# Two layers of attention on one core: both layers divide by the softmax sum by way of DMA, with the product of the second layer on VectorE

## The chip, the core and the metric

The kernel runs on one core of a Trainium2 chip, in one launch. The metric is the time of an execution on the device in microseconds (us). An execution that is profiled has a time of its own, and the span of its records, from the first instruction to the last, is a little shorter. The engines are named as in the profile: PE is TensorE (matmuls and transposes), PEld its loads of weights, DVE is VectorE, ACT is ScalarE, POOL is GpSimd, SP is SyncE, which here only issues DMAs. PE works at full or at reduced clock; the profile gives the clock that was granted as a share of the full one.

## The reference

The input x has B = 2 sequences of T = 2048 tokens with D = 256 features, in fp32. Two layers follow one another, each of the same shape:

```python
for layer in (0, 1):
    xn = layernorm(x)
    s  = attention(xn)          # 16 heads of 16 features, then W_o and b_o (layer 0: + xn)
    g  = silu(ffn(xn))
    x  = x + s * g
```

The attention of layer 0 is full: every query sees all 2048 keys, with scale 1/16. The attention of layer 1 is local: query i sees key j where |i - j| <= 64, with scale 1/4. In both, softmax(q k^T) v is computed per head, the heads are put side by side and multiplied with W_o. The ffn of layer 0 is a mixture of eight products of projections with a running sum over the tokens; that of layer 1 is one linear map plus eight gated low-rank ones. The change leaves the ffn parts alone.

## The kernel before

All activations are held with features on the 128 partitions and tokens along the free axis. The 256 features are two chunks (NC = 2), the tokens of one sequence are four blocks of TB = 512 (NB = 4). The kernel has four stages: preparation, layernorm and ffn of layer 0 (0 to 475 us), attention of layer 0 (to 2141), layernorm and ffn of layer 1 (to 2246), attention of layer 1 (to the end).

**Attention (L402, called once for each layer).** The 16 heads are four groups (g) of NG = 4. A group of four heads stands in one tile: each head has 32 partitions (HP), of which 16 (HD) hold its features. In the tiles of q and k the row after these features is used too: in k it holds ones, in q minus the largest score of that query, so that the score matmul (32 rows deep) already yields the score less its maximum. In v a column of ones is added, so that the weighted sum also yields, in row 16 of each head's 32, the softmax sum by which the result has to be divided.

The work is cut into 32 items (b, g, n): one sequence, one group of heads, one block of 512 queries. An item has U steps: 16 in layer 0 (one per 128 keys), 2 in layer 1 (one per 256 queries with their neighbouring keys). For an item the maxima come first: PE computes scores into `sq` (L599), DVE reduces them (L611 in layer 0; in layer 1 L606, which adds a mask and takes the maximum in one pass). `place_max` (L630) turns the maxima with a PE transpose (`pmx`, L636), negates them on DVE (`row`, L638), and four DMAs put them into the q tile (L640). LEAD = 3 steps later the scores are computed again, `sk` (also L599), ACT takes the exponential (L615), in layer 1 POOL masks four tiles a step (affine select, L620), and DEL steps later (1 in layer 0, 2 in layer 1) `weigh` (L648) multiplies with v: 16 or 24 small matmuls into `acc` (L662), which ACT copies and, in layer 0, POOL adds up into `av` (L673).

**The order of the work** is written out by hand. The main loop (L824) goes through the steps; in each it issues the scores of the second pass of step s and of the first pass of step s + U + LEAD, the weighted sum of step s - DEL, and then what a table holds for step s. The table is filled by `at(step, function, item)` (L778). Instructions wait for each other only where they use the same tile. Before step 0 the loop has U + LEAD steps with first-pass scores alone; in these the query, key and value jobs of the second sequence (`pp`, L446 and L459) are spread, after an eighth of them has been issued ahead of the loop. Some instructions are pinned with `keep_in_program_order`: a scheduler orders the others of an engine.

**q and k** are computed for all heads of a sequence (`keys_queries`, L442), written to DRAM (`qd`, L451) and fetched by group (`fetch`, L509): for q and k each four DMAs of 16 rows (L519), and one more that sets row 16 of each head in q to zero (L521, from `zd`). POOL memsets have given the tiles their ones and zeros beforehand (L427 on).

**The division in layer 0** (L716 to L753): at hops of 0, 2, 4, 5, 7 and 11 steps after an item, `compact` stores the four rows of softmax sums in DRAM (`rd`) and moves the 4 x 16 rows of values into `xn`, where the features of two groups fill 128 partitions; `invert` loads the sums as 128x16 (`dn`) and takes the reciprocal on DVE (L733); `spread` writes it back to DRAM and loads it as 64x512, each row 16 times (`recb`, L744); `divide` multiplies on POOL (L753). For the last group of a block `project` (L756) follows at hop 13: 4 matmuls with W_o in two halves (`pr`, L761), product with the gate on DVE (`upd`, L766), sum into x on POOL (L767).

**The division in layer 1** (L681 to L706): `normalize` transposes av on PE in four pieces (`tr`, L687), so that tokens stand on partitions and a softmax sum is one column per head; DVE takes the reciprocal (L689) and multiplies (L690) into a tile with tokens on partitions. For the last group of a block `features` transposes two chunks back with four PE transposes each (`of`, L703), ACT copies them to SBUF (L705), and `project` follows.

Of the kernel before, what the change touches and what calls it, by code (L numbers as in the profile page):

```python
# [13 lines left out]
ALU = mybir.AluOpType  # L14
# [23 lines left out]
def two_layers(ctx: ExitStack, tc: tile.TileContext, a, out):  # L38
# [114 lines left out]

    with tc.tile_pool(name="fw", bufs=1) as fw:
# [90 lines left out]
        nc.vector.memset(ones, 1.0)  # L245

# [155 lines left out]
    def attention(A, scale, local, final):  # L402
# [14 lines left out]
        with ExitStack() as st:  # L417
            pool = lambda name, bufs, **kw: st.enter_context(tc.tile_pool(name=name, bufs=bufs, **kw))
            kq, vp, dr = pool("kq", 1), pool("vp", 1), pool("dr", 1, space=bass.MemoryType.DRAM)
            qd = dr.tile([2, B, D, T], F32, name="qd")  # L420
# [3 lines left out]
            zd = dr.tile([NG, T], F32, name="zd")  # L424

            rd = [[dr.tile([NG, TB], F32, name=f"rd{i}{k}", tag=f"rd{i}{k}") for k in range(2)] for i in range(2)]
            for t in qs:  # L427
                nc.gpsimd.memset(t, 0.0)
            for t in vs + ks:
                nc.gpsimd.memset(t, 1.0)  # L430
            nc.sync.dma_start(out=zd, in_=qs[0][:NG, :])
# [10 lines left out]
            def keys_queries(b, n, i, hf, bank, place):  # L442
                w, bias = ((A["k"], A["bk"]), (A["q"], A["bq"]))[i]
                ps = bank()
                for c in range(NC):
                    nc.tensor.matmul(  # L446
                        ps, w[:, c, bass.ts(hf, P)], xn[b][:, c, bass.ts(n, TB)], start=(c == 0), stop=(c == NC - 1)
                    )
                sb = place()
                nc.scalar.activation(sb, ps, AF.Identity, bias=bias[:, hf : hf + 1])  # L450
                nc.sync.dma_start(out=qd[i, b, bass.ts(hf, P), bass.ts(n, TB)], in_=sb)  # L451
# [57 lines left out]
            def fetch(bg, lo=0, hi=T):  # L509

                if bg >= B * NG:
                    return
                b, g = divmod(bg, NG)
                k0, k1 = max(lo - PAD, 0), (T if hi == T else hi - PAD)
                for i, t in ((1, qs[bg % 2]), (0, ks[bg % 2])):
                    to, s = (slice(lo, hi), slice(lo, hi)) if i else (slice(PAD + k0, PAD + k1), slice(k0, k1))
                    for j in range(NG):
                        h = g * NG + j
                        nc.sync.dma_start(out=t[j * HP : j * HP + HD, to], in_=qd[i, b, h * HD : (h + 1) * HD, s])  # L519

                nc.sync.dma_start(out=qs[bg % 2][HD:P:HP, lo:hi], in_=zd[:, lo:hi])  # L521
# [108 lines left out]
            def place_max(i):  # L630

                b, g, n = items[i]
                q = tiles(i)[0]
                mx, _ = part.pop(i)
                ps = pm.tile([NG * TT, P], F32, name="pmx", tag="m")
                nc.tensor.transpose(ps, mx.rearrange("p j t -> p (j t)"), ident)  # L636
                row = mp.tile([NG * TT, P], F32, name="row", tag="row")
                nc.vector.tensor_scalar(row, ps, -1.0, None, ALU.mult)  # L638
                for j in range(NG):
                    nc.sync.dma_start(  # L640
                        out=q[j * HP + HD : j * HP + HD + 1, bass.ts(n, TB)].rearrange("o (t c) -> o t c", c=P),
                        in_=row[j * TT : (j + 1) * TT, :],
                    )
# [4 lines left out]
            def weigh(i, u, es):  # L648

                b, g, n = items[i]  # L650
                if u == 0:
                    avs[i] = op.tile([P, TB], F32, name="av", tag="av", bufs=2)
# [22 lines left out]
            def heads(b, n):  # L675

                return xn[0 if local else b].rearrange("p c t -> p (c t)")[:, bass.ts(n, TT * D)].rearrange(
                    "p (t h w) -> p t h w", h=H, w=HD
                )

            def normalize(i):  # L681

                b, g, n = items[i]
                av = avs.pop(i)
                ps = pm.tile([P, TT, NG, HP], F32, name="tr", tag="m")
                for t in range(TT):
                    nc.tensor.transpose(ps[:, t].rearrange("p j w -> p (j w)"), av[:, bass.ts(t, P)], ident)  # L687
                rec = op.tile([P, TT, NG], F32, name="rec", tag="rec", bufs=2)
                nc.vector.reciprocal(rec, ps[:, :, :, HD])  # L689
                nc.vector.tensor_tensor(  # L690
                    heads(b, n)[:, :, g * NG : (g + 1) * NG, :], ps[:, :, :, :HD],
                    rec[:, :, :, None].to_broadcast([P, TT, NG, HD]), ALU.mult,
                )

            feats = {}

            def features(i, c):

                b, g, n = items[i]
                ot = heads(b, n).rearrange("p t h w -> p t (h w)")  # L700
                ps = pm.tile([P, TB], F32, name="of", tag="m")
                for t in range(TT):
                    nc.tensor.transpose(ps[:, bass.ts(t, P)], ot[:, t, bass.ts(c, P)], ident)  # L703
                f = op.tile([P, TB], F32, name="f", tag=f"f{c}", bufs=2 if local else 1)
                nc.scalar.copy(f, ps)  # L705
                feats[b, n, c] = f  # L706

            def together(b, g, n):


                lo = g % 2 * NG * HD
                return xn[b][lo : lo + NG * HD, g // 2, bass.ts(n, TB)]

            divs = {}

            def compact(i):  # L716

                b, g, n = items[i]
                av = avs.pop(i)
                nc.sync.dma_start(out=rd[i % 2][0], in_=av[HD:P:HP, :])  # L720
                for j in range(NG):
                    nc.sync.dma_start(out=together(b, g, n)[j * HD : (j + 1) * HD, :], in_=av[j * HP : j * HP + HD, :])

            def flat(d):
                return d.rearrange("j (r e) -> (j r) e", r=P // NG)

            def invert(i, step):

                if step == 0:
                    divs[i] = op.tile([P, NG * TB // P], F32, name="dn", tag="dn", bufs=2)  # L730
                    tc.keep_in_program_order(nc.sync.dma_start(out=divs[i], in_=flat(rd[i % 2][0])))
                else:
                    tc.keep_in_program_order(nc.vector.reciprocal(divs[i], divs[i]))  # L733

            def spread(i, step):

                b, g, n = items[i]
                if step == 0:
                    tc.keep_in_program_order(nc.sync.dma_start(out=flat(rd[i % 2][1]), in_=divs[i]))
                    return  # L740
                recb = op.tile([P, TB], F32, name="recb", tag="recb", bufs=2)
                lo = g % 2 * NG * HD
                for j in range(NG):
                    tc.keep_in_program_order(nc.sync.dma_start(  # L744
                        out=recb[lo + j * HD : lo + (j + 1) * HD, :], in_=rd[i % 2][1][j, :].partition_broadcast(HD)
                    ))
                divs[i] = recb[lo : lo + NG * HD, :]

            def divide(i):

                b, g, n = items[i]
                tc.keep_in_program_order(
                    nc.gpsimd.tensor_tensor(together(b, g, n), together(b, g, n), divs.pop(i), ALU.mult)  # L753
                )

            def project(i, oc):  # L756
# [3 lines left out]
                for c in range(NC):  # L760
                    nc.tensor.matmul(  # L761
                        pr, A["o"][:, c, bass.ts(oc, P)], feats[b, n, c] if local else xn[b][:, c, cols],
                        start=(c == 0), stop=(c == NC - 1),
                    )
# [13 lines left out]
            def at(s, f, *args):  # L778
                after.setdefault(s, []).append((f, args))

            for i, (b, g, n) in enumerate(items):
                at(i * U - LEAD, place_max, i)
                end = (i + 1) * U
                if local:
                    at(end + DEL, normalize, i)
                    if g == NG - 1:
                        for c in range(NC):
                            at(end + DEL + 1 + c, features, i, c)
                        for oc in range(NC):
                            at(end + DEL + 3 + oc, project, i, oc)  # L790
                else:

                    for r, (f, *step) in enumerate(
                        ((compact,), (invert, 0), (invert, 1), (spread, 0), (spread, 1), (divide,))
                    ):
                        at(end + DEL + (0, 2, 4, 5, 7, 11)[r], f, i, *step)
                    if g == NG - 1:
                        for oc in range(NC):
                            at(end + DEL + 13 + oc, project, i, oc)
# [152 lines left out]
def _attn_arrays(l, wq, wk, wv, bq, bk, bv, wo_t, bo):  # L952

    cols = lambda v: np.asarray(v).reshape(NC, P).T
# [4 lines left out]
        f"wo{l}": np.asarray(wo_t).T,  # L959
        f"bq{l}": cols(bq),  # L960
        f"bk{l}": cols(bk),
        f"bv{l}": cols(bv),
# [56 lines left out]
```

## Time and profile before

| | us |
|---|---|
| median of 3 runs | 2621.34 (2620.46 to 2621.35) |
| the profiled execution | 2619.84 |
| span of its records | 2618.1 |
| PE busy | 2570.3 (98%) |
| DVE busy | 1671.5 (64%) |
| ACT busy | 1641.1 (63%) |
| POOL busy | 894.9 (34%) |
| mean granted clock of PE | 0.991 of full |

The times of an engine are those in which it was busy with an instruction other than waiting or issuing. A line of a group reads: line, engine, operation, result and operands with their shapes, count, then busy time and the mean of one in ns, then the idle time of the engine just before them and who ended it. A line of the chain reads: start in us, duration in us, engine, result and line, count; the chain is the work that ended last, followed back from the end, so each piece is what the next one waited for.

### The profile page before, as it was taken

To read this page: it belongs to the slowest core of one execution; us is meant where nothing else is said; L and a number is where in the kernel's file an instruction comes from. 1 tells how busy PE (TensorE), PEld (TensorE's weight loads), DVE (VectorE), ACT (ScalarE), POOL (GpSimd) and SP (SyncE) were. 2 spreads that over 40 slices of the span, in tenths; PEclk is the share of its full clock that TensorE was granted. 3 is DMA by queue.
4 is the path that set the end of the run, shared out by engine and by line. 5 is a ranking of instruction groups with operands and counts; after the bars stand their busy time and mean duration, and the time that the engine had idled before them with its cause. 6 is when DMAs were issued, how large, how long until landed. Compare 5 with 4: busy or idle time off the path is not lost.

```text
span 2618.1 us, 49275 instructions
## 1 busy us (share of the span) xinstructions
PE 2570.3 (98%) x19060; PEld 1099.6 (42%) x19060; DVE 1671.5 (64%) x2753; ACT 1641.1 (63%) x3200; POOL 894.9 (34%) x845
## 2 busy tenths in 40 slices
PE   8999999999999999999999999999999978999999
PEld 5444444543333333333333333333333324558776
DVE  4133332167888888888777888888888523228884
ACT  5300000228888888888778888888888854236655
POOL 0000000203444444444444444444444430206666
PEclk9999999999999999999999999999999989989999
DMA  4031110410001010010010010010000012411120
GB/s 150 3 88 45 53 45 32 99 64 4 8 12 19 8 24 9 6 25 8 6 25 8 6 25 8 6 27 6 8 8 6 10 30 35 96 67 39 46 58 35
DMA packets 58857, 82.08 MB, mean 31 GB/s; under 512 B 24160, under 2 KB 29152, under 8 KB 57040
## 3 DMA queue, kind: packets, MB, share of 16 engines
q1 hardware_dynamic: 56576, 77.36, 12.3%
q8 instruction: 150, 2.46, 0.4%
q10 hardware_dynamic: 2048, 1.58, 0.2%
q14 instruction: 83, 0.68, 0.1%
HBM read 52.22 MB, written 21.95 MB: 28 GB/s over the span
## 4 chain that ended last, share of the span: by engine, by line
PE 97%; DVE 1%; ACT 1%; DMA 0%; issue 0%; POOL 0%; SPq 0%; POOLq 0%; ACTq 0%; DVEq 0%
PE sk L599 25%; PE acc L662 22%; PE sq L599 19%; PE pp L446 4%; PE py L377 4%; PE po L357 4%; PE px L373 4%; PE ph L263 2%; PE pr L761 2%; PE pp L459 2%; PE psf L199 1%; PE po L909 1%; PE tr L687 1%; PE xb L127 1%; PE po L389 1%; PE xt L104 1%
## 5 line engine op out<-in xcount | busy, mean ns | idle before, releaser
L611 DVE TENSOR_REDUCE part<-sq 128x2 f32<-128x1024 f32 x1024 | 1206.7, 1220 | 304.2 <-PE sq L599 303.7
L615 ACT ACTIVATE e<-sk 128x512 f32<-128x512 f32 x2048 | 1062.7, 615 | 214.9 <-PE sq L599 192.2
L599 PE MATMUL sk<-q,k 32*128 32x512 f32 (+2 forms) x5632 | 1149.7, 533 | 0.6 <-ACT e L615 0.4
L599 PE MATMUL sq<-k,q 32*128 32x512 f32 (+2 forms) x5120 | 1140.8, 572 | 3.2 <-DVE part L611 1.7
L673 POOL TENSOR_TENSOR av<-av,more 128x512 f32<-128x512 f32 x480 | 607.7, 1266 | 961.2 <-ACT more L672 961.1
L599 PEld LDWEIGHTS sk<-q,k 32*128 32x128 f32 x5632 | 532.3, 184 | 581.1 <-ACT e L615 490.9
L662 PE MATMUL acc<-e,v 128*32 128x512 f32 x4096 | 550.6, 605 | 0.0
L599 PEld LDWEIGHTS sq<-k,q 32*128 32x128 f32 x5120 | 412.5, 184 | 28.0 <-DVE part L611 14.0
L672 ACT COPY more<-acc 128x512 f32<-128x512 f32 x480 | 287.8, 600 | 3.8 <-PE acc L662 1.7
L662 PEld LDWEIGHTS acc<-e,v 128*32 128x32 f32 x4096 | 82.4, 108 | 391.5 <-ACT e L615 387.0
L393 ACT ACTIVATE gt<-po 128x512 f32<-128x512 f32 x16 | 9.5, 596 | 324.6 <-PE po L389 324.6
L606 DVE CUSTOM_DVE_ANT_0 seen<-sq,mask 128x256 f32<-128x256 f32 (+1 forms) x512 | 177.4, 411 | 41.5 <-PE sq L599 32.8
L399 POOL TENSOR_TENSOR x<-x,up 128x512 f32<-128x512 f32 x16 | 20.2, 1264 | 416.4 <-DVE up L396 416.4
L620 POOL TENSOR_SCALAR_AFFINE_SELECT xn<-xn 128x512 f32<-128x512 f32 x172 | 103.1, 635 | 119.3 <-ACT xn L615 117.4
L381 DVE TENSOR_TENSOR xs<-we,px 128x512 f32<-128x512 f32 x64 | 43.8, 685 | 135.4 <-PE px L373 135.4
L373 PE MATMUL px<-xn,FV 128*128 128x512 f32 x256 | 121.2, 595 | 0.0
L377 PE MATMUL py<-cum,FW 128*128 128x512 f32 x256 | 120.5, 593 | 0.6 <-DVE cum L346 0.6
L615 ACT ACTIVATE xn<-sk 128x512 f32<-128x512 f32 x172 | 90.1, 601 | 48.2 <-PE sk L599 12.9
L357 PE MATMUL po<-pr,UO 128*128 128x512 f32 x256 | 119.0, 592 | 0.0
L383 DVE TENSOR_TENSOR pr<-xs,py 128x512 f32<-128x512 f32 x64 | 44.0, 687 | 62.4 <-PE py L377 62.2
L766 DVE TENSOR_TENSOR upd<-gt,pr 128x512 f32<-128x512 f32 x32 | 22.0, 687 | 86.0 <-PE pr L761 79.5
L357 PEld LDWEIGHTS po<-pr,UO 128*128 128x128 f32 x256 | 48.6, 190 | 61.2 <-issue 60.7
(169 smaller groups left out, 1683.2 us busy)
## 6 DMA issues: line engine op xcount, KB each, us to landing
we<-wd SPq DMA_DIRECT2D x128, 128.0 KB
qd<-sb SPq DMA_DIRECT2D x48, 256.0 KB
k<-qd SPq DMA_DIRECT2D x40, 128.0 KB
q<-qd SPq DMA_DIRECT2D x40, 128.0 KB
x<-in_x SPq DMA_DIRECT2D x8, 512.0 KB
q<-row SPq DMA_DIRECT2D x256, 2.0 KB
xn<-av SPq DMA_DIRECT2D x128, 32.0 KB
recb<-rd SPq DMA_DIRECT2D x128, 32.0 KB
```

What stands on the lines that cost most here:

```text
L357: nc.tensor.matmul(po[oc], UO[:, ch, bass.ts(oc, P)], pr, start=(ch == 0), stop=False)
L373: nc.tensor.matmul(px, FV[:, c, bass.ts(ch, P)], xn[b][:, c, cols], start=(c == 0), stop=(c == NC - 1))
L377: nc.tensor.matmul(py, FW[:, c, bass.ts(ch, P)], cum[:, c, :], start=(c == 0), stop=(c == NC - 1))
L446: nc.tensor.matmul(ps, w[:, c, bass.ts(hf, P)], xn[b][:, c, bass.ts(n, TB)], start=(c == 0), stop=(c == NC - 1))
L599: nc.tensor.matmul(o, lhs, rhs, start=True, stop=True)
L606: nc.vector.tensor_tensor_reduce(seen[:, lo:hi], sq[:, d, t * 2 * P + lo : t * 2 * P + hi], mask[:, lo:hi], 1.0, LOWEST, ALU.add, ALU.max, ...
L611: nc.vector.tensor_reduce(pt[:, pair[0] : pair[1] + 1, t, kb], sq, AX.X, ALU.max)
L615: nc.scalar.activation(e, t, AF.Exp, scale=scale)
L620: nc.gpsimd.affine_select(out=e[:, :, c, :], in_=e[:, :, c, :], compare_op=ALU.is_ge, fill=0.0, base=0, pattern=[[0, 4], [sign, P]], chann ...
L662: nc.tensor.matmul(acc[hp[j], o : o + hi - lo], vs[b][:, kt, vcols(g, j)], es[j][:, lo:hi], start=(r == 0), stop=(r == len(parts) - 1), sk ...
L672: nc.scalar.copy(more, acc)
L673: nc.gpsimd.tensor_tensor(avs[i], avs[i], more, ALU.add)
```

## The change

Layer 1 now divides as layer 0 does, by DMA, and layer 0's DMAs are put together into fewer ones:

- `away` stores the whole tile av (four heads of 32 rows) in DRAM; `compact` loads the softmax sums from there as 128x16 and the 64 rows of values into `xn`, with one DMA each; `invert` takes the reciprocal, `write` stores it, `spread` loads it 16 times over with one DMA, `divide` multiplies. That one DMA can place the four heads, the rows are taken value by value (first value of the four heads, second value of the four heads, and so on): the rows of W_o and the value bias are put in this order on the host (`apart`).
- The hops are 0, 1, 3, 4, 5, 7 with the projection at 8 in layer 1, and 0, 2, 4, 5, 7, 11 with the projection at 13 in layer 0.
- The product stands on DVE in layer 1 and on POOL in layer 0.
- The last item of layer 0 and the last three of layer 1 are divided on PE: `last_there` is the former transposition with reciprocal and product, `last_back` turns the result back with four matmuls against the identity, and ACT copies 64 rows into `xn`. The projection follows at hop 2.
- `qd` is made once, for both layers, with 32 rows per head; eight DMAs of 1 MB in the preparation fill the rows beside the features with ones (k) and zeros (q). `fetch` takes q and k of a group with one DMA each, of 128 rows. The memsets of the q and k tiles on POOL, and `zd`, go.
- `place_max` stores the maxima with one DMA in place of four. `av` has three buffers in layer 1.

```diff
@@ preparation
+            for i, t in ((0, ones), (1, zeros)):
+                for half in range(NC):
+                    nc.sync.dma_start(
+                        out=qd[i, b, bass.ts(half, H // NC), HD:, :], in_=t[:, None, :].to_broadcast([P, NB, TB])
+                    )
...
@@ fetch
-                    for j in range(NG):
-                        h = g * NG + j
-                        nc.sync.dma_start(out=t[j * HP : j * HP + HD, to], in_=qd[i, b, h * HD : (h + 1) * HD, s])
-
-                nc.sync.dma_start(out=qs[bg % 2][HD:P:HP, lo:hi], in_=zd[:, lo:hi])
+                    nc.sync.dma_start(out=t[:, to], in_=qd[i, b, bass.ts(g, NG), :, s].rearrange("h w t -> (h w) t"))
...
@@ place_max
-                for j in range(NG):
-                    nc.sync.dma_start(
-                        out=q[j * HP + HD : j * HP + HD + 1, bass.ts(n, TB)].rearrange("o (t c) -> o t c", c=P),
-                        in_=row[j * TT : (j + 1) * TT, :],
-                    )
+                nc.sync.dma_start(out=q[HD:P:HP, bass.ts(n, TB)].rearrange("j (t c) -> j t c", c=P), in_=row)
...
@@ division
+            def away(i):
+                pin(nc.sync.dma_start(out=ad[i % 3].rearrange("j w f -> (j w) f"), in_=avs.pop(i)))
...
+            def compact(i):
+                divs[i] = op.tile([P, NG * TB // P], F32, name="dn", tag="dn", bufs=3)
+                pin(nc.sync.dma_start(out=divs[i], in_=flat(ad[i % 3][:, HD, :])))
+                pin(nc.sync.dma_start(out=together(*items[i]), in_=ad[i % 3][:, :HD, :].rearrange("j d f -> d j f")))
+            def invert(i):
+                pin(nc.vector.reciprocal(divs[i], divs[i]))
+            def write(i):
+                pin(nc.sync.dma_start(out=flat(rd[i % 3]), in_=divs[i]))
+            def spread(i):
+                lo = items[i][1] % 2 * NG * HD
+                recb = op.tile([P, TB], F32, name="recb", tag="recb", bufs=2)
+                divs[i] = recb[lo : lo + NG * HD, :]
+                pin(nc.sync.dma_start(out=divs[i], in_=rd[i % 3][None, :, :].to_broadcast([HD, NG, TB])))
+            def divide(i):
+                b, g, n = items[i]
+                pin(
+                    (nc.vector if local else nc.gpsimd).tensor_tensor(together(b, g, n), together(b, g, n), divs.pop(i), ALU.mult)
+                )
...
+            def last_back(i):
+                b, g, n = items[i]
+                lo = g % 2 * NG * HD
+                o = divs.pop(i).rearrange("p t d j -> p t (d j)")
+                ps = pm.tile([P, TB], F32, name="of", tag="m")[lo : lo + NG * HD, :]
                 for t in range(TT):
+                    nc.tensor.matmul(ps[:, bass.ts(t, P)], o[:, t], ident, start=True, stop=True)
+                nc.scalar.copy(together(b, g, n), ps)
...
@@ table
+                hops = (0, 1, 3, 4, 5, 7, 8) if local else (0, 2, 4, 5, 7, 11, 13)
+                steps = (away, compact, invert, write, spread, divide)
+                if i >= len(items) - (3 if local else 1):
+                    hops, steps = (0, 1, 2), (last_there, last_back)
+                for hop, f in zip(hops, steps):
+                    at(end + DEL + hop, f, i)
+                if g == NG - 1:
+                    for oc in range(NC):
+                        at(end + DEL + hops[-1] + oc, project, i, oc)
```

## The prediction

> **What bounds the kernel now.** I read the busy shares and the chain that ended last first, to see which engine has to get shorter.
>
> ```profile
> PE 2570.3 (98%) x19060; PEld 1099.6 (42%) x19060; DVE 1671.5 (64%) x2753; ACT 1641.1 (63%) x3200; POOL 894.9 (34%) x845
> PE 97%; DVE 1%; ACT 1%; DMA 0%; issue 0%; POOL 0%; SPq 0%; POOLq 0%; ACTq 0%; DVEq 0%
> ```
>
> The end is set by PE (TensorE) nearly everywhere, so the change pays where it takes instructions from PE, closes a gap in PE's work or ends a stretch at half clock. The division of layer 0 (475 to 2141 us) already runs on DMA and POOL beside PE; only its last item shows. So I looked at layer 1 and at the last item of layer 0, each by its own stretch of the chain.
>
> Layer 1, a steady stretch of the chain:
>
> ```profile
> 2379.75 1.07 PE acc L662 x24
> 2380.83 0.59 PE tr L687 x4
> ...
> 2386.90 1.08 PE acc L662 x24
> 2387.98 0.59 PE tr L687 x4
> ```
>
> The four transposes of an item stand on the chain, at 0.59 us. From one to the next is 7.15 us; over eleven items, from the second copy into av at 2370.28 to the one at 2449.16, it is 7.17. But VectorE is close behind. Groups of 2340 to 2450:
>
> ```profile
> L606 DVE CUSTOM_DVE_ANT_0 seen<-sq,mask 128x256 f32<-128x256 f32 (+1 forms) x232 | 80.1, 410 | 11.0 <-PE sq L599 7.7 <-PE sk L599 3.1 <-issue 0.2
> L690 DVE TENSOR_TENSOR xn<-tr,rec 128x256 f32<-128x256 f32 x12 | 5.1, 424 | 0.4
> ```
>
> An item has sixteen masked maxima, started 0.345 us apart in the timeline (2.76 per step of eight), so 5.52, and 0.27 (row) + 0.28 (reciprocal, to the next start) + 0.42 (product) = 6.5 of its 7.17.
>
> **The change, part by part.**
>
> *Layer 1's transposes, steady part.* Removed per item: tr 0.59 on PE, reciprocal and product, 0.70, on VectorE. Added on VectorE: a reciprocal of 128x16 (0.25, L733 in layer 0) and a product of 64x512 in SBUF (0.69 by the nearest row, L766's 128x512 product, 687 ns). VectorE then has 5.52+0.27+0.25+0.69 = 6.73; PE alone would need 7.17−0.59 = 6.58. So VectorE becomes the longer one by a little, and how much depends on the one operation with no equal in the trace: a product of two SBUF tiles while POOL runs masks. Nearest is L396, which also reads two SBUF tiles:
>
> ```profile
> 215.06 2.64 DVE L396 SCALAR_TENSOR_TENSOR up<-xn,bo,gt 128x512 f32<-128x512 f32 x2 [2.13 <-ACT gt L393]
> 215.89 1.26 POOL L399 TENSOR_TENSOR x<-x,up 128x512 f32<-128x512 f32 x1 [40.94 <-DVE up L396]
> ```
>
> Two of 0.75 each took 2.64: the second ended only after POOL's sum of 1.26 had (1782 ns at most in its row). The Trainium skill says why ("SBUF — State Buffer", section "Who interferes with whom"): a VectorE instruction with two SBUF inputs and a GpSimd instruction that reads SBUF exclude each other for its whole length. The removed product read PSUM and was free of this; the new one meets POOL's masks (L620: 0.635 each, four in a burst of 2.40 per step, POOL busy 0.60 of this stretch). By the row alone without POOL the product costs 0.69. By the rule it waits for what POOL is doing: half a mask in 0.60 of the cases, 0.2; one whole mask, 0.64; a whole burst, 2.40. I take 0.25, since one blocked L396 waited for one instruction and not for a queue of them. The item becomes 6.98 plus some 0.07 of coupling to PE, 7.05: 0.12 less, for the 24 items outside the projections 2.9 us. Bounds: PE-bound at 6.58 gives 14; a whole mask each time gives 7.4, a loss of 6; a burst each time is a rival below.
>
> *The DMAs of layer 1.* Each item issues five: av out, the divisors and the values back, reciprocals out, reciprocals spread. SP holds little in this stretch: the DMA share is 0.14 of 2340 to 2450. The reciprocal stands two steps after its load (7 us, against a landing of 1.7 in layer 0's chain), the product two after the spread. They are hidden; if not, VectorE stands at the pinned reciprocal, the next maxima queue behind it and PE waits for free score banks. Merging four row stores into one relieves SP and nothing that ends late.
>
> *Items with a projection.* The four of b = 0 are bound by PE (46.89 busy of the 47 us from 2460 to 2507). Each loses 0.59 of tr and two blocks of L703 at 0.58: 1.75, times 4 is 7.0 us; the two ACT copies go too, off the path.
>
> *Layer 1's end.* From 2578 on the chain has five tr blocks (2 at 0.59, 3 at 0.44: 2.5) and eight of L703 (2 at 0.58, 6 at 0.44: 3.8). The last three items keep tr (1.5) and get a return of four matmuls each (0.87, an estimate: twice the 0.44 of four transposes, as these are plain fp32 matmuls). 6.3−1.5−2.6 gives 2.2 less; bounds 0 to 4.
>
> *Layer 0's end.* The chain:
>
> ```profile
> 2123.94 1.27 POOL av L673
> 2125.23 0.53 SPq L720
> ...
> 2128.32 1.70 DMA dn<-rd
> ...
> 2133.05 1.80 DMA recb<-rd
> ...
> 2135.18 1.27 POOL xn L753
> ...
> 2136.49 2.09 PE pr L761 x2
> ```
>
> PE stands 11.89 us and comes back at half clock (granted 0.50 from 2130 to 2142). Instead, from 2125.3: tr 0.5, reciprocal and product 0.7, return 0.9, copy 0.6, with gaps 3.0, so the projection starts at 2128.3, not 2136.5: 8.2 less. Its four matmuls took 3.78 at half clock and 1.98 just before; I count 1.3 of the two for a clock kept. 9.5 in all; bounds 7 (clock lost anyway) to 11.
>
> *Layer 1's start.* The built order of instructions differs here: before, four steps' score blocks for the maxima stand one behind the other; after, query, key and value jobs stand between them.
>
> ```profile
> 2305.91 1.09 PE sq L599 x16
> ...
> 2308.54 10.74 PE sq L599 x48
> 2319.29 15.76 PE pp L446 x32
> ```
>
> The 13.4 us from 2305.91 to 2319.29 are four blocks that need 4×1.09 = 4.4 of PE; PE waits for VectorE to free the score banks. The granted clock falls to 0.53 and 0.50 (2309 to 2319) and stays low into the jobs: 15.76 for eight, where eight at 1.72 are 13.8. With jobs of over 4 us between the blocks, VectorE's 2.85 per block is covered: 9.0 + 2.0 = 11. Against it stands the new fetch: whole 128-row tiles of 1 MB each for q and k, twice the bytes (padding travels too), and the first sq comes earlier. The old ones were issued from 2271.8 to 2285.8. At 144 to 246 GB/s (2324 to 2330, 2142 to 2146) the first group's 2 MB take 8 to 14 us, which from 2284, among the last old issues, is 2292 to 2298; the first sq would be wanted at about 2296. I take off 2, which leaves 9; bounds 0 and 12.
>
> *Nothing expected:* the eight 1 MB stores of ones and zeros, early, beside the preparation's PE work (if they delay a weight load, a few us); layer 0's fetches, far ahead; the memsets on POOL that go; layer 0's five DMAs for eleven, same steps.
>
> **Sum.** 2.9 + 7.0 + 2.2 + 9.5 + 9 = 30.6. The profiled execution took 2619.84 (span 2618.1), 1.5 below the median of 2621.34; taken from the median, 2590.7. 0.2%, about 5.2 us, is what a measurement of this kernel can tell from no change.
>
> **The rivals.**
>
> *VectorE is held by POOL.* If a product waits 0.6 to 1.2, the item is 7.4 to 8.0: the steady part loses 6 to 20 where I have a gain of 2.9, which gives 2600 to 2613. For it: the 1782 ns; against it: POOL rests 1.2 us between bursts.
>
> *Slower than before.* The same product waits for whole bursts, 2.40 each: 6.73+2.40+0.07 = 9.2 per item, 24×2.03 = 49 lost, against 27.7 gained elsewhere: 2643. It decides where the loss reaches 27.7: 1.16 per item, an item of 8.33, a mean wait of about 1.5. Against it: POOL's instructions too would have to wait their turn, and VectorE asks once a mask ends.
>
> *Layer 1's start doesn't gain.* The tiles come 9 us late; PE stands at the first sq. 2599.7. For it: doubled bytes. Against: the second group's 2 MB may come later, and DMA is at 0.39 of its time even in the fuller stretch of 2306 to 2309.
>
> *VectorE costs nothing,* its product falls in POOL's pauses and PE bounds at 6.6: 10 to 11 more, 2580.
>
> **How the numbers follow.** Forecast 0.50 (own range 2583 to 2598); POOL holds VectorE 0.15, of which 0.04 end within 0.2%; slower 0.08; late tiles 0.15; free product 0.12. Faster is 0.50+0.11+0.15+0.12 = 0.88, the same 0.04, slower 0.08. Low 2577 takes in most of the free product with a good end of layer 0; high 2612 most of the held one; outside stay the bursts and some of each tail.
>
> **What would show it.** Right: pr of layer 0's end at about 2128 with clock near 1; no block of 48 sq at layer 1's start, and clock near 1 there; items of layer 1 at 7.0 to 7.1, with PE waiting some tenths per item for VectorE; the L717 products at 0.7 to 1.3. Wrong: L717 above 1.8; PE idle for k or q near 2296, or for the divisors' DMA; a longer preparation.

## The result and the profile after

The changed kernel takes 2596.11 us (median of 4 runs, 2593.54 to 2599.59), the kernel before 2621.35: a ratio of 0.9905 (95% interval 0.9891 to 0.9920), 25 us less. Forecast were 2590.7, so 31 less. The profiled execution has a span of 2594.0, against 2618.1. The page of the changed kernel, engines and chain:

```profile
PE 2543.6 (98%) x18916; PEld 1075.1 (41%) x18916; DVE 1681.6 (65%) x2755; ACT 1633.7 (63%) x3188; POOL 893.3 (34%) x836
PE 93%; DVE 3%; DMA 2%; ACT 1%; issue 1%; POOL 0%; POOLq 0%; ACTq 0%; SPq 0%; DVEq 0%
PE sk L605 24%; PE acc L664 21%; PE sq L605 18%; PE pp L456 4%; PE py L391 4%; PE po L371 4%; PE px L387 4%; PE pr L750 2%; PE ph L277 2%; PE pp L469 2%; PE psf L204 1%; DVE seen L612 1%; PE po L893 1%; DMA q<-row 1%; PE xb L127 1%
```

PE's share of the chain fell from 97 to 93%. VectorE and DMA have come in: 3 and 2%, among them the DMA `q<-row`, which the chain of before does not name.

To see where the time went I cut both executions at the same pieces of work: the end of the last sum into av in layer 0 (2125.21 before, 2123.37 after), the first transpose of layer 1's layernorm (2141.56, 2132.68), and in layer 1 the second copy into av of item 0 (2363.00, 2341.68), of item 5 (2398.95, 2374.39) and of item 28 (2581.72, 2558.99).

| stretch | forecast | change in the traces |
|---|---|---|
| up to layer 0's last sum into av | 0 | -1.8 |
| layer 0's end, to the first transpose of the layernorm | -9.5 | -7.0 |
| from there to item 0 of layer 1 | -9 | -12.4 |
| items 1 to 28 of layer 1 | -9.9 | -1.4 |
| of these items 1 to 5 | | -3.2 |
| and items 6 to 28 | | +1.8 |
| from item 28 to the end | -2.2 | -1.4 |
| sum | -30.6 | -24.1 |

The first row is no finding: the executions of the first three experiments with the changed kernel, which have the same code up to that layernorm, reach its first transpose between 2132.64 and 2135.69. The large difference is in layer 1's items. Its first five, before a product runs on VectorE, gain; the sixth to the 28th together are slower than before. Items 7 to 12 take 7.26 to 7.43 us each, where they took 6.88 to 7.35. The five items over which projections are spread (14 to 18 before, 17 to 21 after) take 2.6 us less even so; the steady ones lose more than that.

The chain of the changed kernel in layer 1 (start, duration, what):

```profile
2397.87 1.13 DVE xn L717
2398.99 0.03 issue
2399.03 0.25 DVE dn L701
2399.28 0.13 DVE row L644
...
2400.72 4.88 DMA q<-row
2405.60 0.14 issue
2405.74 0.48 PE sk L605 x2
```

The product (L717), the reciprocal (L701) and only then the row of negated maxima (L644) follow one another on VectorE; then the row's DMA, issued 1.3 us after the row is made, takes 4.88 us, and PE waits for it. Groups and waits from 2378 to 2450 (a wait: engine and line, what was waited for, us in total, times, longest):

```profile
L605 PE MATMUL sk<-q,k 32*128 32x128 f32 (+1 forms) x478 | 45.6, 315 | 4.1 <-DMA q<-row 2.0 <-DVE row L644 1.5 <-ACT av L669 0.3
L605 PEld LDWEIGHTS sk<-q,k 32*128 32x128 f32 x474 | 37.5, 185 | 10.8 <-DVE row L644 3.9 <-ACT av L669 2.8 <-ACT xn L621 1.5
L626 POOL TENSOR_SCALAR_AFFINE_SELECT xn<-xn 128x512 f32<-128x512 f32 x52 | 34.5, 696 | 12.7 <-ACT xn L621 12.1 <-PE sq L605 0.6
```

```profile
2378.00:2450.00 72.00, 67.34 (x1284) 52.61 (x1276) 66.17 (x347) 47.36 (x101) 52.24 (x80) 1.00 0.51 153
```

And a steady stretch before:

```profile
2387.00:2450.00 63.00, 62.65 (x1172) 51.00 (x1174) 55.98 (x311) 41.74 (x89) 42.27 (x71) 1.00 0.16 44
```

These two lines give the stretch, its length and the busy times in it: after the change PE 67.34 of 72, then PEld, VectorE 66.17, ACT, POOL, then the clock, the DMA share and GB/s. Before, PE was busy 62.65 of 63; now neither PE nor VectorE is full. PE waits for `row` in two ways: `pmx`, its source, lies in one of the four PSUM banks that `sk` also takes in turn (tag m), so the bank is free only when VectorE has made the row; and `sk` needs the row in q. The DMA share rose from 0.16 to 0.51. The queue that issues these DMAs stands too, in the same stretch:

```profile
SPq L711 <- DMA rd<-dn: 21.0, 10, 3.7
```

SP waits 21.0 of 72 us at the spread of the reciprocals (L711) until their store has landed, and what follows on SP, the loads and the next row, waits with it.

The end of layer 0 and the start of layer 1 in the chain:

```profile
2123.42 0.67 PE tr L725 x4
...
2124.41 0.62 DVE over L729
...
2125.16 1.53 PE of L742 x8
2126.69 3.10 PE pr L750 x4
...
2129.88 0.70 DVE upd L755
...
2132.68 1.11 PE xt L104 x8
```

```profile
2287.32 0.97 PE sq L605 x16
2288.29 10.50 PE pp L456 x24
2298.78 1.08 PE sq L605 x16
2299.86 10.50 PE pp L456 x24
2310.36 1.08 PE sq L605 x16
```

No block of 48 `sq` is left, and the granted clock is 1.00 from 2280 to 2340, where before it fell to 0.51 (2309 to 2319).

### The profile page after: what moved, and what is told of

Read it like the earlier page. It is cut to its first block, busy times and chain, and to the rows that moved or that the text cites. A ratio compares the mean times of both kernels' runs of the same rounds, so it can differ in the third digit from the quotient of the medians.

```text
span 2594.0 us, 48140 instructions
## 1 busy us (share of the span) xinstructions
PE 2543.6 (98%) x18916; PEld 1075.1 (41%) x18916; DVE 1681.6 (65%) x2755; ACT 1633.7 (63%) x3188; POOL 893.3 (34%) x836
## 4 chain that ended last, share of the span: by engine, by line
PE 93%; DVE 3%; DMA 2%; ACT 1%; issue 1%; POOL 0%; POOLq 0%; ACTq 0%; SPq 0%; DVEq 0%
PE sk L605 24%; PE acc L664 21%; PE sq L605 18%; PE pp L456 4%; PE py L391 4%; PE po L371 4%; PE px L387 4%; PE pr L750 2%; PE ph L277 2%; PE pp L469 2%; PE psf L204 1%; DVE seen L612 1%; PE po L893 1%; DMA q<-row 1%; PE xb L127 1%
## 5 line engine op out<-in xcount | busy, mean ns | idle before, releaser
L605 PEld LDWEIGHTS sq<-k,q 32*128 32x128 f32 x5120 | 403.5, 183 | 22.2 <-DVE part L617 12.2
L626 POOL TENSOR_SCALAR_AFFINE_SELECT xn<-xn 128x512 f32<-128x512 f32 x172 | 110.0, 671 | 90.7 <-ACT xn L621 89.6
```

Of the source, the lines that this page charges most:

```text
L605: nc.tensor.matmul(o, lhs, rhs, start=True, stop=True)
L626: nc.gpsimd.affine_select(out=e[:, :, c, :], in_=e[:, :, c, :], compare_op=ALU.is_ge, fill=0.0, base=0, pattern=[[0, 4], [sign, P]], chann ...
```

## The experiments

All comparisons are with the kernel before, run on the same chip beside them; the changed kernel's ratio is 0.9905.

**Which wait holds up layer 1: the product, the order, the engine?** First the product was left out, then moved behind the row, then given to POOL; a fourth run undid the end of layer 0.

```diff
-                pin(
-                    (nc.vector if local else nc.gpsimd).tensor_tensor(together(b, g, n), together(b, g, n), divs.pop(i), ALU.mult)
-                )
+                if local:
+                    divs.pop(i)
+                    return
+                pin(nc.gpsimd.tensor_tensor(together(b, g, n), together(b, g, n), divs.pop(i), ALU.mult))
```

> The changed kernel with the 29 products of layer 1 on VectorE left out (the values of layer 1 stay undivided; the reciprocals and all DMAs stay). In the changed kernel the first five items of layer 1, before any product, took 6.34 to 6.56 us, those with a product 7.25 to 7.43. Theory A (VectorE's step with product, reciprocal and row is the bound): items stay at 6.5 to 6.7 throughout, some 24 times 0.75 less, 2578. Rival B (the new DMA traffic of layer 1 is the bound, the row of maxima lands late): items stay at 7.2 to 7.4, at most 3 us less, 2593 or more.

2585.62 us, ratio 0.9871 (0.9854 to 0.9887). Most items take 6.53 to 6.75, as theory A says. But single ones, where PE stands for a row issued behind fetches, take up to 9.89 (others 7.59, 7.45, 7.37, 7.24), and the time lies between the two forecasts: the product is one cause, and a second is left.

```diff
-                for f, args in after.get(s, []):
+                for f, args in sorted(after.get(s, []), key=lambda t: local and t[0] is not place_max):
```

> The changed kernel with the row of maxima issued first in its step in layer 1, so that it stands ahead of the product and the reciprocal on VectorE and ahead of the loads on SP's queue. Theory A1 (the row is late behind the product, holds one of the four score banks and its DMA starts late, so PE waits): PE's waits for the row and for its DMA go, the item is VectorE's 6.96 busy plus little, 7.0 to 7.1, some 7 us less, 2589. Theory A2 (only VectorE's total counts, with the product at 0.92): items stay at 7.3, 2595 to 2597. Rival B (traffic): the single stalls of PE for the row's DMA shrink, 3 to 5 us less, the other items stay.

2578.73 us, 0.9839 (0.9824 to 0.9853): the product stays, and the kernel is faster than without it. Steady items take 6.30 to 6.99. From 2378 to 2450 PE's waits for the row are gone:

```profile
2378.00:2450.00 72.00, 71.14 (x1410) 56.49 (x1406) 70.59 (x384) 51.71 (x110) 56.94 (x87) 1.00 0.55 164
```

PE is busy 71.14 of 72 us, VectorE 70.59. This is A1's sign, with twice its gain: A1 took VectorE's 6.96 per item for its least, and that is too much. In two items of four, 4 of the 16 maxima are over 192 columns and not 256 (0.28 from one start to the next and not 0.345), and the products themselves got shorter: their median is 723 ns here, 921 in the changed kernel.

```diff
-                    (nc.vector if local else nc.gpsimd).tensor_tensor(together(b, g, n), together(b, g, n), divs.pop(i), ALU.mult)
+                    nc.gpsimd.tensor_tensor(together(b, g, n), together(b, g, n), divs.pop(i), ALU.mult)
```

> The changed kernel with the products of layer 1 on POOL, as in layer 0. VectorE then has 6.0 per item, PE 6.58, POOL 8 masks of 0.635 and one product of 1.28, 6.4. Theory A: items of 6.6 to 6.8, some 16 us less, 2580. If the masks behind a product hold up PE's weighted sums, items of 7.0 to 7.2, 2588 to 2592. Rival B: no change, 2596.

2586.62 us, 0.9870 (0.9855 to 0.9884). Like the run without product: items of 6.53, and in between 9.64, 7.73, 7.22, 7.87, 8.40. There PE waits for the row's DMA (2378 to 2450):

```profile
PE sk L605 <- DMA q<-row: 9.3, 5, 3.4
```

The fourth:

```diff
-                if i >= len(items) - (3 if local else 1):
+                if local and i >= len(items) - 3:
```

> The changed kernel with the last item of layer 0 divided by DMA and POOL like the others (hops to 11, projection at 13), layer 1 as changed. The prediction gave the division on PE at this place 9.5 us; the two traces show 7.0 from the last sum into av to the first transpose of the layernorm. By the trace: 2603; by the prediction's step: 2605.5; if the gap is filled by other work: no change, 2596.

2602.36 us, 0.9928 (0.9912 to 0.9943): 6.2 more than the changed kernel, near the 2603 that the traces gave (the intervals of the two ratios overlap a little). The chain goes through four DMAs of 1.8 to 2.4 us, and the transposes of the layernorm start at 2138.53.

**What makes the row's DMA late?** With the product on POOL, only this is left to explain. The runs of this part all have the product on POOL, as in the third run, unless the text says otherwise; the diffs show what comes on top. First the fetches were put behind the row, by pinning the row's DMA and then theirs.

```diff
-                    at(end, fetch, b * NG + g + 2, 0, T // 2)
+                    at(end + 1, fetch, b * NG + g + 2, 0, T // 2)
...
-                    at(end, fetch, b * NG + g + 2, T // 2 if local else 0)
+                    at(end + (1 if local else 0), fetch, b * NG + g + 2, T // 2 if local else 0)
...
-                for f, args in after.get(s, []):
+                for f, args in sorted(after.get(s, []), key=lambda t: local and t[0] is fetch):
...
-                nc.sync.dma_start(out=q[HD:P:HP, bass.ts(n, TB)].rearrange("j (t c) -> j t c", c=P), in_=row)
+                rd_ = nc.sync.dma_start(out=q[HD:P:HP, bass.ts(n, TB)].rearrange("j (t c) -> j t c", c=P), in_=row)
+                if local:
+                    tc.keep_in_program_order(rd_)
...
-                    nc.sync.dma_start(out=t[:, to], in_=qd[i, b, bass.ts(g, NG), :, s].rearrange("h w t -> (h w) t"))
+                    fd = nc.sync.dma_start(out=t[:, to], in_=qd[i, b, bass.ts(g, NG), :, s].rearrange("h w t -> (h w) t"))
+                    if local and bg > 1:
+                        tc.keep_in_program_order(fd)
```

> The run with the product on POOL, and in layer 1 the two fetches of half a group (0.5 MB each) issued one step later and held behind the row of maxima in SP's order; PE's and VectorE's orders are the same as in that run. Its items of 9.64, 7.73, 7.22, 7.87, 8.40 and 7.74 us stand where a fetch was issued just ahead of a row, against 6.53 elsewhere. Theory C1 (the row's DMA lands late behind those fetches): these items fall to 6.5 to 6.7 and some 9 us go, 2577. Theory C2 (it is late behind the loads of the divisors and of the values): unchanged, 2585 to 2588.

2589.38 us, 0.9880 (0.9865 to 0.9896): no gain. The long items are other ones (7.73, 10.48, 8.16, 8.61, 7.75). SP's queue shows why; the timeline (start, duration, what):

```profile
2377.41 0.44 SPq L527 DMA_DIRECT2D k<-qd  x1
2377.89 0.60 SPq L708 DMA_DIRECT2D rd<-dn  x1
2378.54 0.59 SPq L692 DMA_DIRECT2D ad<-av  x1
2383.57 0.55 SPq L715 DMA_DIRECT2D recb<-rd  x1
2384.21 0.76 SPq L701 DMA_DIRECT2D dn<-ad  x1
2385.03 0.59 SPq L702 DMA_DIRECT2D xn<-ad  x1
2385.71 0.58 SPq L647 DMA_DIRECT2D q<-row  x1
```

After the fetch, the store of the reciprocals (`rd<-dn`) is issued at 2377.89, and SP stands until 2383.57 before it can issue the spread that needs it. The next row is issued only after that, at 2385.71. So C1's forecast fails here, and C2 names the neighbours but not the cause. I formed C3: the row is late because it is queued on SP behind an instruction that waits for another DMA to land. Then the row was put first in its step:

```diff
-                for f, args in after.get(s, []):
+                for f, args in sorted(after.get(s, []), key=lambda t: local and t[0] is not place_max):
```

> The run with the product on POOL, and the row of maxima first in its step: ahead of the reciprocal on VectorE and of the loads of divisors and values on SP, but still behind the fetches. Theory C1 (the fetches delay the row's DMA): the long items stay, shortened by the 1 to 1.5 us that the row is issued earlier, 2580 to 2584. Theory C2 (the loads delay it): they go, all items at 6.5 to 6.7, 2577. Both: faster than the changed kernel with the row first (2578.7) only if VectorE was its bound.

2574.99 us, 0.9823 (0.9805 to 0.9840). The row still comes behind fetches, but ahead of spread and loads, and no long item is left: outside the projections 6.30 to 6.78. By items and time this is the forecast of C2 (and of C3). SP stands here too, 17.2 of 72 us, but at the row itself, which it issues 0.03 us after the row is made.

```profile
2378.00:2450.00 72.00, 71.45 (x1409) 57.05 (x1401) 64.90 (x374) 51.56 (x110) 66.65 (x101) 1.00 0.61 175
```

It is the fastest version of the study, with a DMA share higher (0.61) than where the rows came late.

To see what VectorE's order alone is worth, the row was put first on VectorE while its DMA kept its place, in a function of its own; the product is on VectorE here:

```diff
+            def put_max(i):
+                b, g, n = items[i]
+                q = tiles(i)[0]
+                row = rows_.pop(i)
                 nc.sync.dma_start(out=q[HD:P:HP, bass.ts(n, TB)].rearrange("j (t c) -> j t c", c=P), in_=row)
...
                 at(i * U - LEAD, place_max, i)
+                at(i * U - LEAD, put_max, i)
...
-                for f, args in after.get(s, []):
+                for f, args in sorted(after.get(s, []), key=lambda t: local and t[0] is not place_max):
```

> The changed kernel with the row of maxima ahead of the product and the reciprocal on VectorE in layer 1, while its DMA keeps its place on SP behind the loads of divisors and values (of every second pair of fetches one half now comes behind it). Theory A1 (PE waits because the row, late on VectorE, holds one of the four score banks): items of 7.3 to 7.4 fall to 6.7 to 6.8 except where a fetch is in front, 2580 to 2584. If the place on SP made the whole gain of the run with the row first: 2592 to 2596.

2578.23 us, 0.9838 (0.9823 to 0.9853). Items fall to 6.3 to 6.96, with one of 7.93; it equals the run with the row first on both. So A1 holds: with the product on VectorE the order there makes nearly the whole gain, and a row that is ready earlier is no longer late by its place on SP except once, by 1.5 us. The two halves of a fetch lie slightly apart in this build, so a part may come from that.

The next run takes the kernel before and changes the way of fetching alone, with what belongs to it (the stored ones and zeros; the memsets of the q and k tiles go).

```diff
+    qd = ctx.enter_context(tc.tile_pool(name="qd", bufs=1, space=bass.MemoryType.DRAM)).tile(
+        [2, B, H, HP, T], F32, name="qd"
+    )
...
-                    for j in range(NG):
-                        h = g * NG + j
-                        nc.sync.dma_start(out=t[j * HP : j * HP + HD, to], in_=qd[i, b, h * HD : (h + 1) * HD, s])
-
-                nc.sync.dma_start(out=qs[bg % 2][HD:P:HP, lo:hi], in_=zd[:, lo:hi])
+                    nc.sync.dma_start(out=t[:, to], in_=qd[i, b, bass.ts(g, NG), :, s].rearrange("h w t -> (h w) t"))
```

> The kernel before with one part of the change alone: q and k in DRAM with 32 rows a head, the rows of ones and zeros stored in the preparation, and one DMA of 128 rows for each fetch. The built order of PE then has the score blocks at layer 1's start between the query, key and value jobs, as in the changed kernel. If this makes the 12.4 us between the first transpose of layer 1's layernorm and the first item: 2608 to 2610, the rest as before. If that came from the other parts: 2618 to 2621. If the doubled bytes cost something in the steady part of layer 1: between.

2608.85 us, 0.9954 (0.9939 to 0.9969), as forecast. The start of layer 1 has the changed kernel's form,

```profile
2296.63 0.97 PE sq L603 x16
2297.60 10.50 PE pp L454 x24
2308.10 1.08 PE sq L603 x16
```

and item 0's second copy comes at 2351.00 and not 2363.00, of which 0.85 was there at the layernorm's first transpose (2140.71). The items after it keep 6.88 to 7.29: the doubled bytes cost nothing while the rows go by SP without DMA round trips beside them.

**Is it the spread that SP stands at?** Two runs issued it a step later, with the product on POOL and on VectorE.

```diff
-                hops = (0, 1, 3, 4, 5, 7, 8) if local else (0, 2, 4, 5, 7, 11, 13)
+                hops = (0, 1, 3, 4, 6, 8, 9) if local else (0, 2, 4, 5, 7, 11, 13)
```

> The run with the product on POOL, and in layer 1 the spread of the reciprocals one step later (hops 0, 1, 3, 4, 6, 8, projection at 9), so that SP doesn't come to it before their store has landed; the row keeps its place behind the loads and the fetches. Theory C3 (SP stands at the spread until the store of the reciprocals, itself behind a fetch, has landed, and the row's DMA is queued behind it): the long items (9.64, 7.73, 7.22, 7.87, 8.40, 7.74) fall to 6.5 to 6.7, 2576 to 2579. If the fetches or the loads themselves delay the row: unchanged, 2585 to 2588.

> The changed kernel (product on VectorE) with those hops alone: 0, 1, 3, 4, 6, 8, projection at 9. The product now falls on the other step of an item than the row, so that only the reciprocal stands ahead of the row, and SP isn't held at the spread. Theory A1 with C3: items of 6.7 to 6.9, 2576 to 2581. If VectorE's total of the two steps counts alone: 7.3, 2596.

2614.73 us, 0.9977 (0.9967 to 0.9988), and 2616.49, 0.9991 (0.9981 to 1.0001). Both expectations fail. In these two the projection of the first sequence comes so late that its second half reads values which the next sequence has already overwritten, and items 18 to 21, where they meet, take up to 20.57 us; only the items before can be read. There too it got worse: items of 11.57 and 9.74 with POOL, 10.88 and 9.79 with VectorE. SP no longer stands at the spread, but at the next instruction of the same kind:

```profile
SPq L697 <- DMA ad<-av: 25.0, 9, 4.2
```

The load of the divisors (L697) now comes to its turn before the store of av has landed, 25.0 of 72 us (with the product on POOL; 26.1 on VectorE), and the row is still behind it. So the narrow form of C3, the spread, falls; the last run, with the former hops, tests the wide one.

```diff
-                nc.sync.dma_start(out=q[HD:P:HP, bass.ts(n, TB)]
+                (nc.scalar if local else nc.sync).dma_start(out=q[HD:P:HP, bass.ts(n, TB)]
```

> The run with the product on POOL, and in layer 1 the row's DMA issued by ScalarE in place of SP; PE's and VectorE's orders are the same, and the loads, stores and fetches stay on SP. Theory C3 in its wide form (the row is late because it is queued on SP behind an instruction that waits for another DMA to land): the long items fall to 6.5 to 6.7, 2575 to 2579. Theory C1 (the row's transfer itself is slow behind the fetches and stores in the DMA engines): the long items stay, 2583 to 2588. If ScalarE's wait for the row holds up its exponentials: all items longer, 2590 or more.

2583.31 us, 0.9864 (0.9848 to 0.9881). From 2378 to 2450 SP still stands at the spread,

```profile
SPq L711 <- DMA rd<-dn: 19.9, 10, 4.9
```

but PE doesn't wait for the row any more. The long items before the projections are gone: those of 9.64, 7.73, 7.22, 7.87 and 8.40 us are 6.71, 6.71, 6.71, 6.73 and 6.70. So the items do what C3 says, although the time lies in the range forecast for C1. In return the other items are 6.55 to 6.79 where they were 6.53 (ScalarE waits 6.9 us for products on POOL in this stretch; what of it is due to the DMA wasn't separated). From item 0 to item 31 the traces give 3.5 us less than the run with the product on POOL (218.7 against 222.2); by the ratios the two can't be told apart.

**Two delays that add up.** C1 and C3 are not alternatives. A row's DMA raises its semaphore once about 1 us after its issue and then four times more; in the chain PE is released by the last of these, so they tell when each row landed. For the rows of items 6 to 26, in us (in the last column PE's waits for the row's DMA from 2360 to 2560):

| run | from row made to its issue | to landing, no fetch in the 2.3 before the issue | to landing, two fetches there | PE waits |
|---|---|---|---|---|
| changed kernel | 0.6 to 3.6 | 2.0 to 2.5 | 4.3 to 5.6 | 5.5 |
| product on POOL | 0.0 to 5.0 | 1.7 to 3.0 | 4.3 to 5.7 | 10.8 |
| the same, fetches behind the row | 0.8 to 5.5 | 1.9 to 2.8 | none | 10.7 |
| the same, row first | 0.03 | 1.7 to 2.0 | 3.2 to 5.5 | 0 |
| the same, row issued by ScalarE | 0.0 to 0.7 | 1.7 to 2.7 | 4.2 to 4.5 | 0 |

The transfer does take 2 to 3 us more behind two fetches (two rows only in the last run), as C1 supposes, and the place on SP costs up to 5.5. With the product on POOL, PE stood at six rows; each was behind two fetches and late on SP too, 6.4 to 8.9 from row made to landing. With the fetches behind the row the transfers are short, but the stay on SP has grown, and PE stood where the sum was 6.0 to 8.1. With the row first or on ScalarE's queue the sum is at most 5.5, and PE never waited. So PE has some 5.5 us for both (an estimate from these sums), and taking away the stay on SP was enough. The transfer alone can be too long as well: in the run with the row first and the product on VectorE one row, issued 0.03 us after it was made, released PE 0.6 late. Its line in the chain, and the longest of the run with the product on POOL:

```profile
2369.99 6.34 DMA q<-row
2384.10 5.70 DMA q<-row
```

## Why the prediction was right and wrong

*Layer 0's end* (forecast 9.5, measured 7.0; 6.2 by the run that undid it). The way to the projection was right: it starts 3.3 us after the last sum into av, forecast 3.0, where it was 11.3. The term "1.3 for a clock kept" failed. The granted clock is 0.62 from 2126 to 2130, the four matmuls took 3.10 against 3.78, and the gate's product (`upd`) starts after all four, at 2129.88, where before it started after two (why, the runs don't show). From the projection to the transposes 6.0 us pass instead of 5.1. The clock's gain came one stage later: the sixteen transposes take 1.97 instead of 3.65.

*Layer 1's start* (forecast 9, measured 12.4, of which those transposes are 1.7). The step held, and the fetch with twice the bytes wasn't late, so the 2 taken off were too careful. The run with this part alone shows that the way of fetching, with what belongs to it, brings the new order and the time.

*Layer 1's end* (2.2, measured 1.4). A return of four matmuls took 1.02, not 0.87.

*The projections* (7.0). The five items over which the projections of the first sequence are spread took 53.7 us before. With the row first and the product on POOL they take 46.0, 7.8 less, where 7.1 were forecast (7.0 and one steady item's 0.1); in the changed kernel they take 51.2, only 2.6 less. The sum of removed PE work was about right, and another wait used most of it up.

*Layer 1's steady items.* The failed step is in the paragraph on the DMAs of layer 1: "They are hidden; if not, VectorE stands at the pinned reciprocal". They were hidden as far as the division goes, but SP was held by their waits, and the row of maxima is queued on SP behind them; behind two fetches its transfer is longer too. I had named who waits for a late division, not what else is behind a waiting DMA on its queue. With it goes "some 0.07 of coupling to PE": the product and the reciprocal stand ahead of the row on VectorE, and PE can't take the bank of `pmx` back until the row is made. Measured, this is 7.4 to about 6.8, some 0.6 an item (the run with the row first on VectorE alone). The step "VectorE becomes the longer one by a little" was right in kind: PE and VectorE are both full once the row is early. Its size was not: sixteen maxima at 0.345 are too much where some are over fewer columns.

*The product under POOL's masks.* I took 0.69 + 0.25 = 0.94; it took

```profile
L717 DVE TENSOR_TENSOR xn<-xn,recb x29: 675/921/1232, 2368.0 to 2579.4; 64x512 f32<-64x512 f32 x29
```

(least, median, most, in ns). The rule of the Trainium skill ("SBUF — State Buffer", section "Who interferes with whom") fits this case: the spread is at most 0.56, below one mask's 0.635, and POOL's masks, 635 ns before, have a mean of 696 in the stretch from 2378 to 2450. With the row first, the product on VectorE has nearly the same least and a median of 723, so most of the 0.25 depends on when the product falls among the masks. A wait for whole bursts, the rival that would have made the kernel slower, didn't occur. But the port isn't what cost the time: with the row first, the product on VectorE is some 4 us slower than on POOL (2578.73 against 2574.99, with intervals of the ratios that overlap), of the 21 that separate the changed kernel from the latter.

The direction and the range were right, and that the total is only 5 to 6 us off is in part luck: the steady items and the projections brought 1.4 of their 9.9, and the start of layer 1 made up for 3.4 of it. In the traces the forecast has 6.5 us too much: 8.5 in layer 1's items, 2.5 in layer 0's end, 0.8 in layer 1's end, less 3.4 at layer 1's start and 1.8 in the row that is no finding.

Another bank for `pmx` was not tried. How much of VectorE's order acts by the bank and how much by the later DMA is therefore only seen in the waits.

## What to carry to other kernels

When work moves from an engine to DMAs, list what is queued behind each of them on the issuing queue: a DMA that waits for another to land holds up every later one, however small and unrelated, and here moving the wait only moved the place at which the queue stands. Put the short transfer that PE needs soonest ahead of the chained ones, or on another queue, and add to its stay there the longer transfer behind large ones: only the sum decides whether PE waits. In the same way a small VectorE instruction that PE waits for belongs ahead of the larger ones of its step: here the row first, on VectorE and on SP, was worth 17 us, more than leaving the product out altogether (10).

## What the runs showed of the hardware

The clock fell after gaps that were short. Windows of the changed kernel at the end of layer 0, with the columns as above:

```profile
2122.00:2126.00 4.00, 1.50 (x10) 1.29 (x11) 0.86 (x2) 0.00 (x0) 1.36 (x2) 0.95 0.02 6
2126.00:2130.00 4.00, 4.00 (x9) 1.84 (x8) 0.12 (x1) 1.86 (x2) 0.00 (x0) 0.62 0.02 4
```

PE was busy 1.50 of 4.00 us, with the longest gap 2.57 us (2120.84 to 2123.42), and in the next four, which it filled, it was granted 0.62. So here a stretch that was only thinly filled cost clock too, in the work after it.

A row of 8 KB landed 2.0 to 2.5 us after its issue when no fetch had been issued just ahead of it, and 4.3 to 5.6 us behind two fetches, in the same steady items of the changed kernel (DMA share 0.51). With the row first and the product on POOL the share was higher, 0.61, and no row was late. So the share says little of what a single small transfer will meet; what was issued just ahead of it says more.
